# Four-stage transformer kernel, first block: sums and second scores ahead of the second QR broadcast, projection one tick later

## The chip, the cores and the metric

The kernel runs on one core of one Trainium2 chip, as one launch. The metric is the device time of that core in microseconds (us). Before the change it is 1303.81 us, the median of three runs (1302.42, 1303.81 and 1315.74).

## What is computed

The input is x, 32 sequences of 128 tokens with 144 channels, and one conditioning vector of 144 values for each sequence. Everything is float32. Four layers follow one another:

```
x = L0(x, cond)  # modulated attention (16 heads of 9, q and k normalised per head) + MLP 144-576-144
x = L1(x, cond)  # U = qr(P) of a 144x64 matrix; R = expm(A(cond)), A antisymmetric 64x64 per sequence
                 # x + ((x U) R - x U) U^T
x = L2(x, cond)  # modulated attention + MLP
x = L3(x, cond)  # modulated attention + mixture of 4 experts, top 2
```

In L0, q and k of each head of 9 values are divided by their standard deviation: y = (variance + eps)^-1/2. The kernel gets y from a guess made on the bit pattern of the variance (half the bits, subtracted from a constant) and three Newton steps.

## The kernel before, in words

**Tiling.** One sequence is one tile of 128 tokens (partitions) by 144 channels. The three attention layers (L0, L2, L3) are three "blocks", called layers 0, 1, 2 in the code, of 32 sequences each; the rotation L1 is done on the way from the first block to the second. The 144 channels are split into a main part of 128 and a rest of 16.

**Ticks and gaps.** The order of the work is written out by hand. A loop over `tick` starts at -6; each tick carries three sequences through attention: s0 = the sequence whose scores are computed with a first, unshifted product (`ps_s`, whose row maxima `nm` are taken by DVE, line 861), s1 = the one of the tick before, whose shifted scores (`ps_w`) go through the exponential on ACT (line 868), and s2 = the one of two ticks before, whose probabilities are multiplied with the values (`weigh`), normalised and projected. Between these fixed steps lie named gaps (a, e, t, stats, b0, b, den, pre1, c, y1, y2, y3, d, z); `fill(tick, gap)` puts into a gap what was registered for it. All engines work off their own instructions in the order in which this loop issues them, and wait for each other by semaphores.

**The order of a tick of the first block, before:** the deferred residual add (`sums_later`, POOL); gap a; e; t; first half of the scores (24 matmuls on PE, two maxima on DVE, two exponentials on ACT); stats; `weigh` (32 matmuls, a copy on ACT); b0; b; den; `sums` (two transposes on PE, reciprocal and a copy on DVE); second half of the scores (as the first); c; `divide_T` (two transposes on PE); y1; `divide` (DVE, makes oT); y2; y3; d; `largest_T` (one transpose, `ps_nm`) and `largest` (DVE, makes q2); z; `project_out` (two matmuls written `ps_pj`, each counted twice in the profile as float32 goes through PE in two passes) and `project_sum` (a product `res_a` on DVE, line 936; the add into x_sb on POOL, line 933, is put off to the start of the next tick).

**The QR in the gaps.** The QR of P is 64 Householder columns, one after the other, and each comes in three pieces (`prep_qr`, lines 318 to 356): piece 1 broadcasts a row of `at` on PE (line 327), squares and sums it on ACT (line 338), takes the root on POOL (line 339) and copies the row on ACT (line 340); piece 2 is five small DVE instructions (lines 342 to 349); piece 3 is the DVE update of `at` (line 353), which the broadcast of the next column reads. In the ticks 0 to 28 of the first block two columns are done in a tick. I call them A and B. `prepare_qr` (line 1196) puts piece 1 of A into gap a, pieces 2 and 3 of A into gap t, piece 1 of B into gap den, piece 2 of B into y1 and piece 3 into y2.

**What else lies in the gaps.** The matrix exponential (`prep_expm`) takes one piece in gap b and one in gap z of each tick until about tick 23; a piece is either a group of 32 or 64 small PE products with an ACT copy, or one or two DVE instructions over 128x1024 elements (the series). The layer norm's statistics (`ln_stats`: two small DVE instructions for each of two sequences, then seven on POOL) lie in gap e; the Newton steps in b, c and y2 on POOL; the MLP of a group of four sequences from ten ticks on after the group's first (`mlp1` in two parts, three 512-wide chunks in gaps stats and b, two chunks in gap d; `mlp2` in gaps b and d of the two ticks behind these).

**PSUM.** All matmul results but the attention output take the next of seven banks in turn; a bank is free again when its readers of seven allocations before are done.

The edit touches `ln_stats` (line 619), `qk0_guess` (line 754), `prepare_qr` (line 1196), the registration of the statistics and transposes of kind m (line 1253 on), and the loop over ticks (line 1368 on).

Of the kernel before, what the change touches and what calls it, by code (L numbers as in the profile page):

```python
# [10 lines left out]
I32 = mybir.dt.int32  # L11
AF = mybir.ActivationFunctionType
ALU = mybir.AluOpType
# [53 lines left out]
def tile_kernel(ctx: ExitStack, tc: tile.TileContext, a: dict, out: bass.AP):  # L67
# [551 lines left out]
    def ln_stats(pairs):  # L619

        n = len(pairs)
        name = "_".join(f"{kind}{s}" for s, kind in pairs)
        mv = small.tile([128, n, 2], F32, tag="mv", name=f"mv_{name}")
        for k, (s, kind) in reversed(list(enumerate(pairs))):
            bs = small.tile([128, 6], F32, tag="st", name=f"st_{kind}_{s}")
            nc.vector.bn_stats(bs, x_sb[:, of(s)[1], :])
            nc.vector.bn_aggr(mv[:, k, :], bs)  # L627
        rs = small.tile([128, 2, n], F32, tag="rs", name=f"rs_{name}")
        nc.gpsimd.tensor_scalar(rs[:, 0, :], mv[:, :, 1], 1.0, EPS, ALU.mult, ALU.add)  # L629
        nc.gpsimd.tensor_tensor(rs[:, 0, :], rs[:, 0, :], neghalf[:, :n], ALU.pow)  # L630
        nc.gpsimd.tensor_scalar(rs[:, 1, :], mv[:, :, 0], -1.0, 0.0, ALU.mult, ALU.add)
        for k, (s, kind) in enumerate(pairs):
            b = of(s)[1]
            minus, r = rs[:, 1, k : k + 1], rs[:, 0, k : k + 1]
            xh = work.tile([128, CM], F32, tag="xh", name=f"xh_{kind}_{s}", bufs=3)
            nc.gpsimd.tensor_scalar(xh, x_sb[:, b, :CM], minus, r, ALU.add, ALU.mult)
            xr = take_xr()
            nc.gpsimd.tensor_scalar(
                xr.rearrange("p (k c) -> p k c", k=4)[:, :, :CR],
                x_sb[:, b, CM:].unsqueeze(1).to_broadcast([128, 4, CR]),  # L640
                minus, r, ALU.add, ALU.mult,
            )
            st[s][f"xh_{kind}"], st[s][f"xr_{kind}"] = xh, xr

    def ln_T(s, kind):
# [108 lines left out]
    def qk0_guess(s):  # L754
        va = st[s]["va"]
        y = small.tile([128, 32], F32, tag="qky", name=f"qky_{s}", bufs=2)
        nc.vector.tensor_scalar(
            y.bitcast(I32), va.bitcast(I32), 1, None, ALU.logical_shift_right
        )
        nc.vector.tensor_scalar(y.bitcast(I32), y.bitcast(I32), -1, RSQRT, ALU.mult, ALU.add)  # L760
        st[s]["y"] = y

    def qk0_newton(s, eng=nc.gpsimd):
# [186 lines left out]
    def project_sum(s):  # L950
        layer, b, g, i = of(s)
        residual(b, st[s].pop("pj"), gr[g]["ga"][:, i, :], f"a_{s}", layer == 0)
# [243 lines left out]
    def prepare_qr(tick, gap):  # L1196


        nonlocal prep_qr, prep_last, qr_rest
        if late is not None:  # L1200
            return
        if qr_rest:
            if tick < 0:
                pieces = {"e": 1, "stats": 2}
            else:

                pieces = {"a": 1, "t": 2, "den": 1, "y1": 1, "y2": 1}
            for _ in range(pieces.get(gap, 0)):
                next(prep_qr)
                qr_rest -= 1  # L1210
        elif prep_qr:
            if next(prep_qr, 0) == 0:
                prep_qr = None
        elif prep_last is None and not prep_expm:
            prep_last = prep_rot(rot_T[0])
        elif prep_last and next(prep_last, 0) == 0:
            load_late()
# [17 lines left out]
    def put(tick, gap, f, *args):  # L1235
        gaps[tick, gap].append((f, args))
# [16 lines left out]
    for layer in range(3):  # L1253
        ahead = 5 if layer == 0 else 6
        for n in range(NG):
            g = (layer, n)
            t0 = first[layer] + n * G
            for i in range(G):
# [6 lines left out]
                    put(at_a - 1, "b", rotate_in, n)  # L1265
                    put(at_a - 1, "d", rotate, n)
                stats[at_a].append((s, "a"))
                stats[t0 + i + 3].insert(0, (s, "m"))
                if layer < 2:
                    put(*((at_a, "d") if at_a != t0 + i - ahead else (at_a + 1, "b")), ln_T, s, "a")  # L1270
                else:
                    put(at_a, "d", ln_T, s, "a")
                if layer == 0:
                    put(t0 + i + 4, "a", ln_T, s, "m")
                else:
                    put(t0 + i + 3, "d", ln_T, s, "m")
                if layer == 0:
# [77 lines left out]
    def fill(tick, gap):  # L1355
        prepare_qr(tick, gap)
        while (tick, gap) == (last_prep, "b0") and late is None:
            prepare_qr(tick, gap)
            prepare_expm(tick, gap)

        if gap == ("t" if tick < 0 else "e" if tick < first[1] else "stats") and tick in stats:
            ln_stats(stats.pop(tick))
        for f, args in gaps.pop((tick, gap), ()):
            f(*args)
        prepare_expm(tick, gap)

    last_prep = first[1] - 5
    for tick in range(-6, first[2] + B + 14):
        s0, s1, s2 = (at_tick.get(tick - k) for k in range(3))
        for layer in range(3):  # L1370
            for n in range(NG):
                if tick == first[layer] + n * G:
                    gr[layer, n]["ga"] = load_gates(layer, n, 0)
                if tick == first[layer] + n * G + (6 if layer else 9):
                    gr[layer, n]["gm"] = load_gates(layer, n, 1)
        while sums_later:
            sums_later.pop()()
        fill(tick, "a")
        fill(tick, "e")
        fill(tick, "t")  # L1380
# [3 lines left out]
            weigh(s2)  # L1384
        fill(tick, "b0")
        fill(tick, "b")
        fill(tick, "den")
        joined = tick >= first[1]
        if s2 is not None and not joined:
            sums(s2)  # L1390
        fill(tick, "pre1")
        if s2 is not None and joined:
            sums_by_blocks(s2)
        scores(s0, s1, 1)
        fill(tick, "c")
        if s2 is not None and not joined:
            divide_T(s2)
        fill(tick, "y1")
# [15 lines left out]
        fill(tick, "z")  # L1414
        if joined:
            fill(tick, "d")
        if s2 is not None and not ahead:
            project_out(s2)
            project_sum(s2)
    assert not gaps and not stats, (sorted(gaps), sorted(stats))  # L1420
# [164 lines left out]
```

## Time and profile before

The profile is of one execution that took 1303.81 us; its span from the first to the last instruction is 1302.1 us, so 1.7 us lie around it. That execution is also the median of the three.

| what | from | value |
|---|---|---|
| PE, DVE, ACT, POOL busy | part 1 of the page | 97%, 62%, 64%, 53% of the span |
| granted TensorE clock, mean | cores view | 0.993 |
| first block, ticks 0 to 28 (37 to 381 us) | broadcasts of line 327 in the timeline | 344 us |
| broadcast of column A to that of B, tick 8 | timeline | 121.00 to 126.15 us |
| broadcast of B to that of the next A, tick 8 | timeline | 126.15 to 131.44 us |
| the guess of the inverse root, two DVE instructions, tick 8 | timeline, lines 757 and 760 | 0.15 and 0.22 us |
| rest of the normalised x, 128x64, POOL | timeline, line 638 | 0.39 us |

The length of each of the ticks 0 to 28, from one broadcast of column A to the next (for tick 28, whose QR column is the last, to the transpose `ps_nm`), in us:

```
tick    0    1    2    3    4    5    6    7    8    9
      11.4 10.5  9.7 12.3 10.6 10.5  9.5  9.5 10.4 10.8
tick   10   11   12   13   14   15   16   17   18   19
      13.3 12.2 12.2 12.1 12.0 14.2 11.5 12.3 13.3 13.7
tick   20   21   22   23   24   25   26   27   28
      13.0 12.9 13.3 13.4 11.0 10.5 12.0 11.4  9.8
```

How to read it: a matmul's end is modelled, so PE counts as busy somewhat longer than it works. Idle time is only shown with what ended it. A line like `[0.97 <-DVE oT L926]` says that the engine had been idle for 0.97 us and that DVE's oT, line 926, set it free. In the waits view a line gives the engine and the line that waited, what for, the sum in us, how often, and the longest.

### The profile page before, as it was taken

The page shows a single profiled execution, that of the slowest core. Times are in us where ns is not written, and L with a number is a line of the kernel's source. Part 1 is how long each engine was busy: PE and PEld are TensorE (multiplying, and loading weights), DVE is VectorE, ACT ScalarE, POOL GpSimd, SP SyncE. Part 2 cuts the span into 40 slices and gives each one's busy share as a digit, 9 for nine tenths or more (in the row PEclk, how much of TensorE's full clock was granted, in tenths as well). Part 3 has the DMA queues.
Part 4 walks back from the last instruction along what each step waited for, and adds up shares of the span by engine and source line. Part 5 has one row for each costly group of instructions (what it writes and reads, how often), then busy time and mean ns, then how long its engine had stood idle before and what let it go on. Part 6 is the DMA issues. An engine that isn't in the chain of part 4 may idle for free.

```text
span 1302.1 us, 35663 instructions
## 1 busy us (share of the span) xinstructions
PE 1259.5 (97%) x14180; PEld 920.3 (71%) x14180; DVE 807.7 (62%) x2534; ACT 833.4 (64%) x1832; POOL 690.4 (53%) x1667
## 2 busy tenths in 40 slices
PE   6989898999999999999999999999999999999998
PEld 4678676786776667767777766767676767677666
DVE  5698888876774457667666666646464646455343
ACT  3568677678767566777767777665656555555431
POOL 5667777665753345445445554746464636361610
PEclk9999999999999999999999999999999999999999
DMA  8200000000003000000110000200000000000000
GB/s 234 62 2 21 20 7 15 20 3 22 20 2 134 19 11 21 11 20 20 37 29 20 20 11 11 76 11 19 11 20 11 19 11 19 11 19 2 19 10 10
DMA packets 21720, 34.43 MB, mean 26 GB/s; under 512 B 2353, under 2 KB 12497, under 8 KB 21297
## 3 DMA queue, kind: packets, MB, share of 16 engines
q1 hardware_dynamic: 20896, 31.70, 8.1%
q8 instruction: 114, 1.87, 0.6%
q10 hardware_dynamic: 656, 0.42, 0.2%
q14 instruction: 54, 0.43, 0.1%
HBM read 29.65 MB, written 2.47 MB: 25 GB/s over the span
## 4 chain that ended last, share of the span: by engine, by line
PE 71%; DVE 3%; ACT 1%; issue 0%; POOL 0%; DVEq 0%; POOLq 0%
PE ps_h L668 19%; PE ps_f L1118 10%; PE ps_s L856 7%; PE ps_qk L668 6%; PE ps_w L856 6%; PE ps_o L883 5%; PE ps_f L977 5%; PE ps_pj L947 3%; PE ps_v L668 2%; PE ps_f L1123 1%; PE ps_o L815 1%; DVE nm L861 1%; PE ps_z L1009 1%; PE ps_hT_m L656 1%; PE ps_cw L1106 1%; PE ps_hT_m L655 1%
## 5 line engine op out<-in xcount | busy, mean ns | idle before, releaser
L861 DVE TENSOR_REDUCE nm<-ps_s 128x4 f32<-128x512 f32 x384 | 246.3, 682 | 89.4 <-PE ps_w L856 67.8
L868 ACT ACTIVATE pr<-ps_w 128x512 f32<-128x512 f32 x384 | 208.6, 595 | 106.1 <-PE ps_w L856 104.6
L856 PE MATMUL ps_s<-kT,qT 32*128 32x256 f32 x1536 | 228.4, 404 | 0.7 <-ACT kT L791 0.6
L856 PE MATMUL ps_w<-q,kT 32*128 32x128 f32 x3072 | 229.0, 283 | 0.0
L856 PEld LDWEIGHTS ps_w<-q,kT 32*128 32x128 f32 x3072 | 194.2, 187 | 9.8 <-issue 6.2
L971 ACT ACTIVATE hid<-ps_h 128x512 f32<-128x512 f32 (+1 forms) x224 | 120.0, 591 | 100.1 <-PE ps_h L668 99.6
L856 PEld LDWEIGHTS ps_s<-kT,qT 32*128 32x128 f32 x1536 | 134.5, 184 | 29.6 <-issue 8.6
L668 PE MATMUL ps_h<-hM_m,mlps 128*128 128x512 f32 x304 | 144.0, 607 | 0.0
L1127 DVE SCALAR_TENSOR_TENSOR acc<-ps_f,cw,acc 128x144 f32<-128x144 f32 x128 | 46.7, 366 | 149.5 <-PE ps_f L1118 74.3
L933 POOL TENSOR_TENSOR x_sb<-x_sb,res_a 128x144 f32<-128x144 f32 x96 | 47.1, 490 | 146.7 <-DVE res_a L936 145.9
L883 PE MATMUL ps_o<-pr,vaug 128*32 128x128 f32 x3072 | 104.2, 276 | 0.3 <-issue 0.3
L883 PEld LDWEIGHTS ps_o<-pr,vaug 128*32 128x32 f32 x3072 | 78.1, 109 | 33.4 <-PE ps_w L856 18.9
L668 PEld LDWEIGHTS ps_h<-hM_m,mlps 128*128 128x128 f32 x304 | 53.3, 189 | 67.5 <-issue 66.6
L734 POOL TENSOR_SCALAR kT<-kT,cst 128x512 f32<-128x512 f32 x40 | 62.4, 1564 | 61.5 <-ACT kT L721 60.5
L977 PE MATMUL ps_f<-mlps,hid 128*128 128x144 f32 x640 | 93.5, 293 | 0.0
L977 PEld LDWEIGHTS ps_f<-mlps,hid 128*128 128x128 f32 x640 | 82.4, 191 | 7.8 <-issue 3.2
L868 ACT ACT_TABLE_LOAD x57 | 73.1, 1283 | 6.5 <-PE ps_w L856 5.7
L629 POOL TENSOR_SCALAR rs_m_a<-mv_m_a 128x2 f32<-128x2 f32 x81 | 15.6, 193 | 114.4 <-DVE mv_m_a L627 86.1
L968 ACT ACT_TABLE_LOAD x58 | 74.4, 1283 | 1.0
L658 ACT ACTIVATE hM_m<-ps_hT_m,modM 128x128 f32<-128x128 f32 x96 | 44.7, 465 | 45.5 <-PE ps_hT_m L656 45.4
L1118 PEld LDWEIGHTS ps_f<-pair,hid 128*128 128x128 f32 x512 | 66.9, 190 | 8.4 <-issue 7.7
L1118 PEld LDWEIGHTS ps_f<-mlps,hid 128*128 128x128 f32 x512 | 66.7, 190 | 8.1 <-issue 7.2
(328 smaller groups left out, 2918.5 us busy)
## 6 DMA issues: line engine op xcount, KB each, us to landing
gates<-gates SPq DMA_DIRECT2D x48, 288.0 KB, 3.5
x_sb<-in_x SPq DMA_DIRECT2D x8, 288.0 KB, 9.2
out_x<-x_sb SPq DMA_DIRECT2D x7, 288.0 KB, 2.5
mlps<-in_L_mlp SPq DMA_DIRECT2D x2, 1000.0 KB, 6.2
pair<-in_L_mlp SPq DMA_DIRECT2D x1, 1800.0 KB, 11.8
mlps<-in_L_mlp SPq DMA_DIRECT2D x1, 1800.0 KB, 8.2
pow<-in_W SPq DMA_DIRECT2D x4, 320.0 KB, 6.5
mlps<-in_L_wmod SPq DMA_DIRECT2D x4, 290.0 KB, 4.8
```

The source lines that it names most:

```text
L668: nc.tensor.matmul(ps, x, y, start=k == 0, stop=k == 1)
L734: eng.tensor_scalar(o, k, m, None, ALU.mult)
L856: nc.tensor.matmul(o, x, y, start=True, stop=True)
L861: nc.vector.tensor_reduce(nmv[:, at0 : at0 + 2, ONE : ONE + 2], view.rearrange("p (r t k) -> p r t k", t=2, k=T), AX.X, ALU.max, negate=True,)
L868: nc.scalar.activation(pr[:, 4 * e : 4 * e + 4, :].rearrange("p s q -> p (s q)"), view, AF.Exp, scale=SCALE,)
L883: nc.tensor.matmul(po[rows4(j), t, :], v[:, 4 * j + 2 * t + r, :], prs[j // 2][:, 4 * (j % 2) + 2 * r + t, :], start=r == 0, stop=r == 1,)
L933: nc.gpsimd.tensor_tensor(x_sb[:, b, :], x_sb[:, b, :], t, ALU.add)
L968: nc.scalar.activation(t, half, AF.Gelu_apprx_tanh)
L971: nc.scalar.activation(hid[:n, i], ps[:n], AF.Gelu_apprx_tanh)
L977: nc.tensor.matmul(ps, hid[:, at0, i, :], w2[:, m, :], start=m == 0, stop=m == NFC - 1)
L1118: nc.tensor.matmul(ps[:, 0, :], hid[:, at0 + m, i, :], w2[:, at0 + m, :], start=m == 0, stop=m == 3)
L1127: nc.vector.scalar_tensor_tensor(acc, ps[:, 0, :], w, acc, ALU.mult, ALU.add)
```

## The change

- The deferred residual add on POOL moves from the start of the next tick to behind gap c.
- In the first block piece 1 of column B moves from gap den to the head of gap c, which lies behind the second half of the scores. `sums` now comes ahead of gap den.
- The projection of the first block is done one tick later (for the sequence of three ticks before instead of two), behind `sums` and ahead of the second scores, instead of at the end of the tick. Statistics and transposes of kind m, which read its sum, are a tick later too (4 and 5 instead of 3 and 4 ticks behind).
- The guess of the inverse root is one DVE instruction (times -0.5, plus constant) instead of two (shift; times -1, plus constant).
- The rest of the normalised x of kind a is written once in the first block (128x16) instead of four times (128x64).

```
--- before.py
+++ after.py
@@ -635,11 +635,12 @@
             xh = work.tile([128, CM], F32, tag="xh", name=f"xh_{kind}_{s}", bufs=3)
             nc.gpsimd.tensor_scalar(xh, x_sb[:, b, :CM], minus, r, ALU.add, ALU.mult)
             xr = take_xr()
-            nc.gpsimd.tensor_scalar(
-                xr.rearrange("p (k c) -> p k c", k=4)[:, :, :CR],
-                x_sb[:, b, CM:].unsqueeze(1).to_broadcast([128, 4, CR]),
-                minus, r, ALU.add, ALU.mult,
-            )
+            if s < B and kind == "a":
+                o, rest = xr[:, :CR], x_sb[:, b, CM:]
+            else:
+                o = xr.rearrange("p (k c) -> p k c", k=4)[:, :, :CR]
+                rest = x_sb[:, b, CM:].unsqueeze(1).to_broadcast([128, 4, CR])
+            nc.gpsimd.tensor_scalar(o, rest, minus, r, ALU.add, ALU.mult)
             st[s][f"xh_{kind}"], st[s][f"xr_{kind}"] = xh, xr
 
     def ln_T(s, kind):
@@ -754,10 +755,7 @@
     def qk0_guess(s):
         va = st[s]["va"]
         y = small.tile([128, 32], F32, tag="qky", name=f"qky_{s}", bufs=2)
-        nc.vector.tensor_scalar(
-            y.bitcast(I32), va.bitcast(I32), 1, None, ALU.logical_shift_right
-        )
-        nc.vector.tensor_scalar(y.bitcast(I32), y.bitcast(I32), -1, RSQRT, ALU.mult, ALU.add)
+        nc.vector.tensor_scalar(y.bitcast(I32), va.bitcast(I32), -0.5, RSQRT, ALU.mult, ALU.add)
         st[s]["y"] = y
 
     def qk0_newton(s, eng=nc.gpsimd):
@@ -1204,7 +1202,7 @@
                 pieces = {"e": 1, "stats": 2}
             else:
 
-                pieces = {"a": 1, "t": 2, "den": 1, "y1": 1, "y2": 1}
+                pieces = {"a": 1, "t": 2, "c": 1, "y1": 1, "y2": 1}
             for _ in range(pieces.get(gap, 0)):
                 next(prep_qr)
                 qr_rest -= 1
@@ -1265,13 +1263,13 @@
                     put(at_a - 1, "b", rotate_in, n)
                     put(at_a - 1, "d", rotate, n)
                 stats[at_a].append((s, "a"))
-                stats[t0 + i + 3].insert(0, (s, "m"))
+                stats[t0 + i + 3 + (layer == 0)].insert(0, (s, "m"))
                 if layer < 2:
                     put(*((at_a, "d") if at_a != t0 + i - ahead else (at_a + 1, "b")), ln_T, s, "a")
                 else:
                     put(at_a, "d", ln_T, s, "a")
                 if layer == 0:
-                    put(t0 + i + 4, "a", ln_T, s, "m")
+                    put(t0 + i + 5, "a", ln_T, s, "m")
                 else:
                     put(t0 + i + 3, "d", ln_T, s, "m")
                 if layer == 0:
@@ -1373,8 +1371,6 @@
                     gr[layer, n]["ga"] = load_gates(layer, n, 0)
                 if tick == first[layer] + n * G + (6 if layer else 9):
                     gr[layer, n]["gm"] = load_gates(layer, n, 1)
-        while sums_later:
-            sums_later.pop()()
         fill(tick, "a")
         fill(tick, "e")
         fill(tick, "t")
@@ -1384,15 +1380,21 @@
             weigh(s2)
         fill(tick, "b0")
         fill(tick, "b")
-        fill(tick, "den")
         joined = tick >= first[1]
         if s2 is not None and not joined:
             sums(s2)
+        s3 = at_tick.get(tick - 3, B)
+        if s3 < B:
+            project_out(s3)
+            project_sum(s3)
+        fill(tick, "den")
         fill(tick, "pre1")
         if s2 is not None and joined:
             sums_by_blocks(s2)
         scores(s0, s1, 1)
         fill(tick, "c")
+        while sums_later:
+            sums_later.pop()()
         if s2 is not None and not joined:
             divide_T(s2)
         fill(tick, "y1")
@@ -1414,7 +1416,7 @@
         fill(tick, "z")
         if joined:
             fill(tick, "d")
-        if s2 is not None and not ahead:
+        if s2 is not None and s2 >= B and not ahead:
             project_out(s2)
             project_sum(s2)
     assert not gaps and not stats, (sorted(gaps), sorted(stats))
```

More of the change, by code (lines that the diff above doesn't have):

```diff
@@ L637, in ln_stats @@
             xr = take_xr()
[L638 to L642, printed above, removed]
+            if s < B and kind == "a":
+                o, rest = xr[:, :CR], x_sb[:, b, CM:]
+            else:
+                o = xr.rearrange("p (k c) -> p k c", k=4)[:, :, :CR]
+                rest = x_sb[:, b, CM:].unsqueeze(1).to_broadcast([128, 4, CR])
+            nc.gpsimd.tensor_scalar(o, rest, minus, r, ALU.add, ALU.mult)
             st[s][f"xh_{kind}"], st[s][f"xr_{kind}"] = xh, xr
@@ L756, in qk0_guess @@
         y = small.tile([128, 32], F32, tag="qky", name=f"qky_{s}", bufs=2)
[L757 to L760, printed above, removed]
+        nc.vector.tensor_scalar(y.bitcast(I32), va.bitcast(I32), -0.5, RSQRT, ALU.mult, ALU.add)
         st[s]["y"] = y
@@ L1205, in prepare_qr @@
             else:
-                pieces = {"a": 1, "t": 2, "den": 1, "y1": 1, "y2": 1}
+                pieces = {"a": 1, "t": 2, "c": 1, "y1": 1, "y2": 1}
             for _ in range(pieces.get(gap, 0)):
@@ L1267, in tile_kernel @@
                 stats[at_a].append((s, "a"))
-                stats[t0 + i + 3].insert(0, (s, "m"))
+                stats[t0 + i + 3 + (layer == 0)].insert(0, (s, "m"))
                 if layer < 2:
@@ L1273, in tile_kernel @@
                 if layer == 0:
-                    put(t0 + i + 4, "a", ln_T, s, "m")
+                    put(t0 + i + 5, "a", ln_T, s, "m")
                 else:
@@ L1375, in tile_kernel @@
                     gr[layer, n]["gm"] = load_gates(layer, n, 1)
-        while sums_later:
-            sums_later.pop()()
         fill(tick, "a")
@@ L1386, in tile_kernel @@
         fill(tick, "b")
-        fill(tick, "den")
         joined = tick >= first[1]
@@ L1390, in tile_kernel @@
             sums(s2)
+        s3 = at_tick.get(tick - 3, B)
+        if s3 < B:
+            project_out(s3)
+            project_sum(s3)
+        fill(tick, "den")
         fill(tick, "pre1")
@@ L1395, in tile_kernel @@
         fill(tick, "c")
+        while sums_later:
+            sums_later.pop()()
         if s2 is not None and not joined:
@@ L1416, in tile_kernel @@
             fill(tick, "d")
-        if s2 is not None and not ahead:
+        if s2 is not None and s2 >= B and not ahead:
             project_out(s2)
```

## Prediction

> **What bounds the kernel now.** The change touches the first block only, so I read the page (parts 1 and 4: PE is busy 97% and makes 71% of the chain that ended last), then the busy time by stretches, then the waits of that block, then single ticks in the timeline.
>
> ```profile
> core 0: us, PE busy (x) PEld busy (x) DVE busy (x) ACT busy (x) POOL busy (x), PEclk, DMA share, GB/s
> 37.00:69.00 32.00, 30.54 (x404) 21.78 (x406) 25.08 (x87) 19.41 (x58) 19.41 (x64) 1.00 0.22 53
> 69.00:142.00 73.00, 67.58 (x1023) 55.71 (x1024) 65.01 (x230) 52.40 (x154) 54.99 (x161) 0.98 0.04 10
> 142.00:381.00 239.00, 225.81 (x3079) 176.20 (x3081) 190.53 (x647) 179.18 (x470) 162.30 (x455) 0.99 0.05 15
> ```
>
> No engine is quite full here: PE idles 20 of 344 us, DVE has 281. From 69 to 142 us DVE is as full as PE. The waits of 37 to 381 us that the edit is after:
>
> ```profile
> PEld ps_pj L947 <- DVE oT L926: 8.6, 7, 1.3
> PE ps_qr L327 <- DVE at L353: 7.8, 6, 2.4
> PE ps_pj L947 <- DVE oT L926: 7.4, 8, 1.1
> DVE st_m L626 <- POOL x_sb L933: 6.0, 26, 0.7
> ```
>
> The first and third are the same stalls seen on PE's two halves: about 8 us for the projection, 8 us for the broadcast, 6 us of DVE. Next, tick 8 (121.00 to 131.44), one answer for each engine. PE, then DVE, ACT and POOL:
>
> ```profile
> 126.15 0.51 PE L327 MATMUL ps_qr<-at,cst 128*128 128x145 f32 x2
> 126.50 0.38 PE L896 MATMUL ps_o<-cst,on 128*128 128x128 f32 x2
> ...
> 127.92 0.66 PE L786 MATMUL ps_qkT<-cst,qkn 128*128 128x128 f32 x4
> ...
> 130.85 0.76 PE L947 MATMUL ps_pj<-L_wproj,oT 128*128 128x144 f32 x4 [0.97 <-DVE oT L926]
> 131.44 0.41 PE L327 MATMUL ps_qr<-at,cst 128*128 128x145 f32 x2
> ```
> ```profile
> 127.97 1.29 DVE L861 TENSOR_REDUCE nm<-ps_s 128x4 f32<-128x512 f32 x2 [0.40 <-PE ps_w L856]
> 129.18 0.15 DVE L342 SCALAR_TENSOR_TENSOR ala<-qrr,qr 128x1 uint32<-128x1 uint32 x1
> ...
> 130.71 0.33 DVE L353 SCALAR_TENSOR_TENSOR at<-qrr,qr,at 128x121 f32<-128x121 f32 x1
> ```
> ```profile
> 126.78 0.29 ACT L338 ACTIVATE qrk<-ps_qr 128x145 f32<-128x145 f32 x1
> ...
> 128.09 1.09 ACT L868 ACTIVATE pr<-ps_w 128x512 f32<-128x512 f32 x2 [0.76 <-PE ps_w L856]
> ```
> ```profile
> 127.24 0.55 POOL L339 TENSOR_TENSOR qr<-qr,half 128x1 f32<-128x1 f32 x1 [0.31 <-ACT qrk L338]
> ```
>
> To be seen: column B's square and root are done (127.79) while PE still computes the second scores and DVE waits for them. DVE starts B's five small instructions (129.18) right behind the two maxima. B's latency is hidden; the tick then ends by DVE: maxima, five instructions, oT, update (131.04), next broadcast.
>
> **The change part by part.** I call "sc" the moment at which PE is through with the second scores (127.92 in tick 8).
>
> *Broadcast B behind the second scores.* Now it starts at sc. ACT's order has the two exponentials ahead of the square: they end at 128.09+1.09 = sc+1.26. The square can overlap by 0.08 (as 129.06, the next ACT row, does); square and read-out take 0.38 (column A in the same tick: 121.51 to 121.89), hand-over 0.08, root 0.55, hand-over 0.28 (A: 122.60 to 122.87): DVE starts at sc+2.47, not at sc+1.26. From there to the end of the update it takes 1.86 as now (129.18 to 131.04), then 0.07: the next broadcast can go at sc+4.40. Before it went at sc+3.52. So DVE idles 1.2 us per tick, and a tick that this chain ends gets 0.88 longer there. Behind the square wait the q and k copies of ACT; behind the root wait eight Newton instructions, the residual add and the variance on POOL (some 1.3+0.5+1.3+0.25), which end at about sc+5.6, so column A's root starts some 0.2 later than its square allows (sc+5.44).
>
> *PE's own work behind sc* sets the end where it is longer than 4.40: broadcast 0.35, ps_qkT 0.49, ps_qk 0.97, rdx 0.22, ps_nm 0.20 = 2.23; and, where the tick has them, an exponential product 1.08, mlp2 1.23, mlp1 2.87 (starts of the rows of ticks 8, 20 and 27).
>
> *First half.* It loses the broadcast (126.15 to 126.50, 0.35) and gets the projection (130.85 to 131.44, 0.59): +0.24. The projection's wait for oT is gone, as oT is a tick old.
>
> *Residual add, statistics.* DVE no longer waits for x_sb (6.0/26 = 0.23 a tick), nor does column A's root stand behind the add, which stands behind res_a, itself behind the 1.0 to 1.3 us series pieces. That only helps where column A's update and the maxima behind it set the pace of the first half, through the banks.
>
> *Guess.* 0.15+0.22 becomes one instruction that the trace does not show; bounds 0.15 and 0.22, I take 0.22 (same form as line 760). *128x16 rest:* between 0.19 (128x2, line 629) and 0.39; I take 0.22, near the small rows. Both gains lie on DVE and POOL beside the chain above: nothing where column B ends the tick, up to 0.3 together where the first half waits for DVE. At worst, 0.
>
> Tick by tick: new end = old sc + 0.24 + the larger of 4.40 and PE's own work.
> - 5, 6, 7, 8 (no MLP): 6.9, 6.0, 5.9, 6.9 + 4.64 = 11.5, 10.6, 10.5, 11.5 against 10.5, 9.5, 9.5, 10.4: **+4.4**.
> - 13, 24, 25, 28 (mlp2 behind sc, no product: 3.46 < 4.40): 0.88+0.24 = 1.12 each: **+4.5**.
> - 10, 14, 18, 22, 26 (mlp1 in the first half, only 2.2 to 3.3 behind sc): here the exponentials also reload their table, 1.28 us, issued when ACT's previous work is done. In tick 14 the previous work ends at 200.21 (199.74+0.47), the exponentials then end at 202.58, 1.7 behind the new sc (200.58-0.25+0.59 = 200.92), not 1.26: +0.4; in 18 and 22 +0.2. So +0.88+0.24+0.3 = 1.4 each: **+7.0**.
> - 12, 16, 17, 20, 21 (PE has 4.54 behind sc with mlp2 and a product, or DVE with its series is the bound): ticks 20 and 21 gain 0.59 and lose 0.60; 12 and 17 gain about 0.4 each from column A, 16 loses 0.1: **-0.5**.
> - 11, 15, 19, 23, 27 (mlp1 behind sc: at least 5.1, so column B is hidden). Column A sets the first half: in tick 11 its DVE start moves from 3.3 to 2.8 behind the broadcast, in 15 from 3.8 to 2.9, in 27 from 2.8 to 2.1, in 19 some 0.6; PE's end loses the projection and gets the broadcast (-0.24). I take -0.7, -2.6, -0.9, 0, -0.8: **-5.0** (tick 15 carries 1.7 of a halved clock, below).
> - 0 to 4 and 9: DVE (matrix set-up) or the modulations are the bound, half of the loss counts: **+1.8**.
> - Ticks 29 to 34: no QR, the projection's stall there (0.8 in tick 28 to 29) and some DVE wait go: **-1**.
>
> Sum: 4.4+4.5+7.0-0.5-5.0+1.8-1 = +11.2 on the profiled execution's 1303.81 (span 1302.1 and 1.7 around it), which is the median: 1315.0.
>
> **The clock.** Rows first: in tick 15 PE stood still and then ran slow.
>
> ```profile
> 209.74 0.30 PEld L327 LDWEIGHTS ps_qr<-at,cst 128*128 128x128 f32 x2 [2.65 <-issue]
> ```
> ```profile
> 210.00:212.00 2.00, 2.00 (x29) 1.61 (x29) 2.00 (x4) 0.67 (x4) 1.83 (x5) 0.80 0.01 4
> 212.00:216.00 4.00, 4.00 (x13) 2.71 (x13) 3.71 (x13) 3.29 (x8) 3.33 (x11) 0.67 0.01 2
> ```
>
> The granted clock fell to a half for about 3.4 us after an idle time of 2.65 us; ps_qkT and ps_qk took 2.83 (211.74 to 214.57) instead of 1.46. That cost about 1.7 with the scores ahead. The new order opens an idle time of 2.2 to 2.5 us at the end of ticks 9, 10, 14 and 26 (4.4 to 4.7 less 2.23). I count none of them in the sum (tick 9 to 10 has a slow stretch already); four would be +6.8.
> The Trainium skill, "TensorE: Matmul & The Clock Gate", section "What's actually happening", has it that the clock halves after an idle window of about 3.4 us. By that rule none of the new idle times would halve it and the sum stays; by the row above, with 2.65 us enough, some will.
>
> **The rivals.**
> - *The clock falls* in three or more of those ticks: +11 and 3 to 5 times 1.7 = 1320 to 1324. For: the row above, and idle times almost as long. Against: 0.97 to 1.24 us idle at the ends of ticks 8, 10 and 14 left the clock whole.
> - *About even*: column A's earlier start is worth more in ticks 9 to 19, where DVE's series makes POOL's add and root late (0.5 more in ten ticks), and ticks 0 to 4 lose nothing: +11-5-2 = 1308, down to 1300.
> - *Faster*: the moved broadcast stays hidden. It decides at sc+1.26: if B's root were there when the maxima are done, the second half would be 0.88 shorter than I have it in about 15 ticks (-13, and -1.5 for the table), and the stalls (8+8) would be free: 1315-14.5-13 = about 1288. For: the waits table. Against: ACT works in order, and its two exponentials end at the very moment at which DVE is done with the maxima; nothing can overtake them.
> - *The change does little*: not possible for the order, it is written out; the waits can only move.
>
> **How the numbers follow.** Forecast (1309 to 1320) 0.50; clock 0.20; even (1297 to 1309) 0.21; faster than 1297 0.09. About 1% is what a measurement of this kernel can tell from no change: 1290.8 and 1316.8. Of the forecast 0.27 lie below 1316.8, 0.23 above. Faster by over 1%: 0.06. Within: 0.27+0.21+0.03 = 0.51. Slower: 0.23+0.20 = 0.43. The range 1301 to 1325 leaves out the "faster" case, some of "even" below it, and a clock that falls more than four times. For the forecast alone it is 1309 to 1320.
>
> **What would show it.** Right: in ticks 5 to 8 DVE idles about 1.2 us between the maxima and line 342, waiting for POOL's root; the exponentials stand ahead of the square; ticks of 11.5 and 10.6; PE idles ahead of broadcast A in ticks 13, 14, 24 to 26; no wait of ps_pj for oT and none of st_m for x_sb; ticks 20 and 21 unchanged at 13. Wrong: ticks 5 to 8 not longer; ticks 11, 15, 27 not shorter; more slow stretches of the clock than before.

## The result, and the profile after

The changed kernel takes 1324.02 us in the median of four runs (1319.52, 1319.77, 1328.27, 1329.04), beside 1306.10 us of the kernel before in four (1302.42 to 1315.74). The ratio is 1.012, with a 95% interval of 1.0077 to 1.0163: some 1% slower (16 us by the ratio, 18 by the medians). The prediction was 1315, and 1301 to 1325 as its range. The profiled execution took 1319.52 us (span 1317.8, granted clock 0.992 against 0.993 before), 15.7 more than that of before.

The busy time by stretches first (columns as in the prediction; the block begins at 36.3 us here, and its tick 28 ends at 389.0 instead of 376.2; so the 37 to 381 us of before hold 4.8 us behind tick 28, its ticks 0 to 28 take 339.3 us together, and tick 28 took 9.6, not 9.8).

```profile
core 0: us, PE busy (x) PEld busy (x) DVE busy (x) ACT busy (x) POOL busy (x), PEclk, DMA share, GB/s
37.00:69.00 32.00, 29.97 (x409) 21.76 (x411) 25.12 (x84) 18.99 (x60) 19.09 (x62) 1.00 0.21 53
69.00:142.00 73.00, 64.57 (x986) 53.52 (x982) 60.25 (x208) 47.61 (x140) 51.60 (x145) 0.95 0.03 10
142.00:389.00 247.00, 227.48 (x3085) 177.72 (x3082) 187.74 (x616) 180.15 (x478) 165.33 (x458) 0.99 0.04 14
```

PE now idles 2.0 + 8.4 + 19.5 = 30 us in these stretches instead of 20 (18.4 up to the end of tick 28); DVE is less full too. So neither got more work: both wait. For what, the waits of 37 to 391 us say:

```profile
POOL qr L339 <- ACT qrk L338: 67.7, 34, 5.8
DVE ala L342 <- POOL qr L339: 28.2, 40, 1.4
PE ps_qr L327 <- DVE at L353: 25.0, 17, 2.6
...
PEld ps_qk L690 <- DVE res_a L934: 4.5, 6, 1.3
...
PE ps_qk L690 <- DVE res_a L934: 3.0, 4, 1.1
```

Two of them before the change:

```profile
POOL qr L339 <- ACT qrk L338: 17.8, 13, 3.6
DVE ala L342 <- POOL qr L339: 2.9, 3, 1.9
```

Read from the bottom of the chain upwards: the broadcast of the next column A (PE, line 327) waits 25.0 us for the update (line 353), where it waited 7.8 before; DVE's five instructions wait 28.2 us for POOL's root (2.9 before), and the root waits 67.7 us for ACT's square (17.8 before; POOL's idle time as such costs nothing). The stalls that the change was after are gone (no wait of `ps_pj` for oT, none of `st_m` for `x_sb`), and a new one has come: `ps_qk` waits for `res_a`, whose product on DVE still holds the projection's PSUM bank.

Tick 8 (123.79 to 135.34), PE, DVE, ACT and POOL:

```profile
130.98 0.51 PE L327 MATMUL ps_qr<-at,cst 128*128 128x145 f32 x2
131.33 0.60 PE L784 MATMUL ps_qkT<-cst,qkn 128*128 128x128 f32 x4
...
132.96 0.27 PE L813 MATMUL ps_nm<-cst,nm 128*128 128x128 f32 x1
135.34 0.59 PE L327 MATMUL ps_qr<-at,cst 128*128 128x145 f32 x2 [2.11 <-DVE at L353]
135.73 0.42 PE L656 MATMUL ps_hT_m<-cst,xh_m 128*128 128x128 f32 x1
```
```profile
131.04 1.29 DVE L859 TENSOR_REDUCE nm<-ps_s 128x4 f32<-128x512 f32 x2 [0.68 <-PE ps_w L854]
133.17 0.20 DVE L342 SCALAR_TENSOR_TENSOR ala<-qrr,qr 128x1 uint32<-128x1 uint32 x1 [0.84 <-POOL qr L339]
```
```profile
131.16 1.08 ACT L866 ACTIVATE pr<-ps_w 128x512 f32<-128x512 f32 x2 [1.44 <-PE ps_w L854]
132.12 0.30 ACT L338 ACTIVATE qrk<-ps_qr 128x145 f32<-128x145 f32 x1
```
```profile
132.59 0.55 POOL L339 TENSOR_TENSOR qr<-qr,half 128x1 f32<-128x1 f32 x1 [2.61 <-ACT qrk L338]
```

To be seen: PE has column B's row ready from about 131.4 on (its next product starts at 131.33), but ACT takes up the square at 132.12, behind the two exponentials; the root ends at 133.14; DVE has waited 0.84; the next broadcast goes at 135.34, 4.36 behind the end of the second scores (130.98), and PE has stood still for 2.11.

All 29 ticks, length after minus length before (us):

```
tick     0     1     2     3     4     5     6     7     8     9
      -0.1   0.0  +0.3  -0.8  +1.0  +1.1  +1.0  +1.0  +1.1  +1.0
tick    10    11    12    13    14    15    16    17    18    19
      +0.4  -0.5  +0.3  +0.7  +1.6  -1.8  +0.4  +0.3  +1.1  -0.4
tick    20    21    22    23    24    25    26    27    28
      +0.1  +0.1  +1.9  -1.0  +0.9  +1.0  +1.6  +0.4  +1.0
```

Sum of ticks 0 to 28 +13.5; the eight ticks behind them +3.5; start and rest of the program -1.2. Together 15.8, the difference of the two executions but for rounding. Three windows of halved clock lie in these ticks of either profile: before in ticks 3, 10 and 15, after in ticks 4, 9 and 27.

### The profile page after: what moved, and what is told of

The parts are those of the page before. It is cut to its first block, busy times and chain, and to the rows that moved or that the text cites. A ratio compares the mean times of both kernels' runs of the same rounds, so it can differ in the third digit from the quotient of the medians.

```text
span 1317.8 us, 35607 instructions
## 1 busy us (share of the span) xinstructions
PE 1261.1 (96%) x14180; PEld 923.2 (70%) x14180; DVE 804.2 (61%) x2502; ACT 830.8 (63%) x1832; POOL 692.5 (53%) x1667
## 3 DMA queue, kind: packets, MB, share of 16 engines
HBM read 29.65 MB, written 2.47 MB: 24 GB/s over the span
## 4 chain that ended last, share of the span: by engine, by line
PE 69%; DVE 3%; ACT 2%; issue 1%; POOL 0%; DVEq 0%; POOLq 0%; ACTq 0%
PE ps_h L669 19%; PE ps_f L1116 9%; PE ps_s L854 7%; PE ps_qk L669 6%; PE ps_w L854 6%; PE ps_o L881 6%; PE ps_f L975 5%; PE ps_pj L945 3%; PE ps_v L669 2%; PE ps_f L1121 1%; PE ps_o L813 1%; DVE nm L859 1%; PE ps_hT_m L656 1%; PE ps_hT_m L657 1%; PE ps_cw L1104 1%
## 5 line engine op out<-in xcount | busy, mean ns | idle before, releaser
L881 PE MATMUL ps_o<-pr,vaug 128*32 128x128 f32 x3072 | 106.9, 281 | 0.1
L881 PEld LDWEIGHTS ps_o<-pr,vaug 128*32 128x32 f32 x3072 | 80.1, 112 | 33.2 <-PE ps_w L854 18.9
L975 PEld LDWEIGHTS ps_f<-mlps,hid 128*128 128x128 f32 x640 | 82.4, 191 | 7.8 <-issue 3.8
L339 POOL TENSOR_TENSOR qr<-qr,half 128x1 f32<-128x1 f32 x64 | 35.0, 548 | 77.5 <-ACT qrk L338 75.7
```

What stands on the lines that cost most here:

```text
L881: nc.tensor.matmul(po[rows4(j), t, :], v[:, 4 * j + 2 * t + r, :], prs[j // 2][:, 4 * (j % 2) + 2 * r + t, :], start=r == 0, stop=r == 1,)
L975: nc.tensor.matmul(ps, hid[:, at0, i, :], w2[:, m, :], start=m == 0, stop=m == NFC - 1)
```

## The experiments

An execution of one and the same kernel varies by some 16 us here (32 runs of the kernel before: 1303.4 to 1319.7). So each experiment is read twice: by its times, and by the ticks of its profile against those of before. "Ticks 1 to 28" is the change of that stretch's sum; tick 0 is left out, as it took 11.2 to 21.0 us in the profiles with the clock's start (in one of them, of 18.9 us, the clock was halved from 30.8 to 54.7 us). The numbers of the kernels below are those of this table's rows.

| kernel | median us | before, same job | ratio, 95% interval | ticks 1 to 28, us |
|---|---|---|---|---|
| 1: column B back in gap den | 1315.1 | 1310.9 | 1.0016 [0.9987, 1.0046] | -1.3 |
| 2: only column B moved | 1326.9 | 1310.9 | 1.0094 [1.0057, 1.0131] | +11.6 |
| 3: changed kernel, square first | 1320.3 | 1310.9 | 1.0061 [1.0037, 1.0084] | +7.6 |
| 4: only the guess and the rest | 1308.4 | 1310.9 | 0.9967 [0.9938, 0.9996] | -4.0 |
| 5: only the late add | 1305.9 | 1310.1 | 0.9960 [0.9933, 0.9988] | -5.0 |
| 6: late add, guess, rest | 1304.3 | 1310.1 | 0.9953 [0.9926, 0.9981] | -7.5 |
| 7: as 6, projection behind the scores | 1302.8 | 1310.1 | 0.9951 [0.9920, 0.9982] | -6.0 |
| 8: as 7, oT behind the update | 1302.4 | 1310.1 | 0.9924 [0.9897, 0.9950] | -2.8 |
| 9: as 8, add behind gap den | 1305.0 | 1310.8 | 0.9959 [0.9930, 0.9988] | -4.9 |
| 10: as 6, add behind gap den | 1304.3 | 1310.8 | 0.9966 [0.9934, 0.9999] | -7.3 |

**Theory:** the loss is column B's broadcast behind the second scores: its square stands behind the exponentials on ACT, and B's latency is no longer hidden. **Rivals:** the loss lies in the projection, in the late add, or in the clock.

**1. Column B back in its old place**, all else as changed.

```diff
-                pieces = {"a": 1, "t": 2, "c": 1, "y1": 1, "y2": 1}
+                pieces = {"a": 1, "t": 2, "den": 1, "y1": 1, "y2": 1}
```

> The changed kernel with one part undone: the broadcast of column B back in gap den, ahead of the second scores; sums first, projection a tick later, short guess and short rest stay. Theory (the moved broadcast exposes column B's latency): nearly all of the loss goes. A tick of the kind of 5 to 8 has the broadcast (0.35) and the projection (0.59) in its first half, sc 0.59 later than in the kernel before, and ends by DVE at sc+3.24 (no projection between): +0.3 against before; ticks 11, 15, 19, 27 stay shorter. Sum 0 to -4 us against before: ratio 0.995 to 1.002, profile near 1303; DVE goes from the maxima straight to line 342. Rival (the later projection and statistics cost the time): it stays 8 us or more above before, ratio over 1.006.

Measured: ratio 1.0016, so most of the loss goes with this one line. But ticks 5 to 8 stay 0.6, 0.3, 0.4 and 0.6 longer than before: something else costs there too. Experiments 6 and 10 name it.

**2. Only column B moved**, all else as before: the same line turned round in the kernel before ("den" to "c").

> The kernel before with that one part done: piece 1 of column B in gap c instead of den; everything else as before. Theory: first half 0.35 shorter; oT is 1.21 later, so the projection runs from about sc+4.14 and the next broadcast goes at sc+4.73 instead of sc+3.52: +0.86 in a tick that column B ends, more in the ticks with a table reload, nothing where PE is full: +10 to +14 us, ratio 1.008 to 1.011. Rival (the projection's place costs the time): within 3 us of before, ratio under 1.003.

Measured: ratio 1.0094, ticks 1 to 28 +11.6. Ticks 5 to 8 get 0.7 to 1.0 longer, ticks 10, 14, 18, 22 and 26 together 6.7; ticks 20 and 21 not at all. The theory holds from both sides: this part alone makes most of the slow-down.

**3. The square ahead of the exponentials.** Column B stays behind the second scores, but piece 1 is issued between their matmuls and their maxima and exponentials, so that ACT does the square first.

```diff
-    def scores(s, w, n):
+    def scores(s, w, n, mid=None):
...
+        if mid is not None:
+            mid()
...
-                pieces = {"a": 1, "t": 2, "c": 1, "y1": 1, "y2": 1}
+                pieces = {"a": 1, "t": 2, "mid": 1, "y1": 1, "y2": 1}
...
-        scores(s0, s1, 1)
+        scores(s0, s1, 1, (lambda: prepare_qr(tick, "mid")) if qr_rest else None)
```

> The changed kernel, but piece 1 of column B is issued between the second scores' matmuls and their maxima and exponentials: on PE it is at the same place, on ACT the square and the row's copy come ahead of the two exponentials. Theory (ACT's order costs most of it): root done at sc+1.55, DVE starts line 342 at sc+1.83 instead of sc+2.47, next broadcast at sc+3.76: -0.64 in ticks that column B ends, -0.9 in those with a table reload; about -10 us against the changed kernel, ratio to before 1.002 to 1.007. Rival (the place on PE behind the scores costs it, whatever ACT does): as the changed kernel, ratio 1.010 to 1.014. Second rival (the later exponentials cost what the square gains, through the q and k copies and the banks): above 1.010 although DVE starts line 342 earlier.

Tick 8 of this kernel on DVE, and ACT from the end of tick 26 into tick 27:

```profile
137.03 1.29 DVE L861 TENSOR_REDUCE nm<-ps_s 128x4 f32<-128x512 f32 x2 [0.68 <-PE ps_w L854]
138.62 0.20 DVE L342 SCALAR_TENSOR_TENSOR ala<-qrr,qr 128x1 uint32<-128x1 uint32 x1 [0.30 <-POOL qr L339]
```
```profile
366.25 0.29 ACT L338 ACTIVATE qrk<-ps_qr 128x145 f32<-128x145 f32 x1 [1.23 <-PE ps_qr L327]
...
366.83 1.28 ACT L868 ACT_TABLE_LOAD   x1
368.12 1.09 ACT L868 ACTIVATE pr<-ps_w 128x512 f32<-128x512 f32 x2
...
370.44 0.46 ACT L746 ACTIVATE qksq<-ps_qk 128x288 f32<-128x288 f32 x1
```

DVE's idle time falls from 0.84 to 0.30, and ticks 5 to 8 are 2.35 shorter together than in the changed kernel. So ACT's order is the cause of about half of the loss there, shown by taking it away. It is all that column B's place costs in these ticks: they stay 1.83 longer than before, and kernel 1, with column B in its old place, keeps 1.91. But the whole kernel gains little (1.0061 against 1.012), and the second answer shows where it is given back: with the square first, the table for the exponential is loaded behind it (366.83), where the changed kernel loads it 0.6 ahead of the end of the second scores (361.26 and 361.87), mostly in ACT's idle time; the exponentials, the q and k copies and the squares `qksq` come later, the variance on POOL waits for these, and the next column A's root stands behind the variance. Ticks 11, 15, 19, 23 and 27 are 5.3 us longer together than in the changed kernel.

**4. Only the guess in one instruction and the 128x16 rest** (those two hunks of the change in the kernel before).

> The kernel before with only the guess in one instruction and the rest of kind a written once. Theory: the new guess takes 0.15 to 0.22 us, so DVE has 0.15 less per tick, POOL 0.2 less; off the path in most ticks: 0 to -3 us, ratio 0.997 to 1.001. Rival (DVE bounds the ticks, so each of its instructions counts): -0.3 in each of 29 ticks, -9 us, ratio 0.993.

Measured: ratio 0.9967. Ticks 11, 12, 16, 17, 19 and 27 get 0.2 to 0.3 shorter, ticks 5 to 8, 13, 14, 18, 20 to 22 and 26 change by less than 0.1: it counts only where DVE's queue or column A is late, as the prediction had it. By the trace the gain is the guess's, one instruction of 0.15 in place of 0.15 and 0.22 (the two parts were not run apart). The rest saves POOL little or nothing: it took 0.35 to 0.39 in 11 ticks and 0.64 in 16, where the 128x64 form took 0.39 to 0.43 and the prediction had 0.22. Tick 8, POOL and DVE:

```profile
139.38 0.64 POOL L643 TENSOR_SCALAR xr<-x_sb,rs_m_a 128x16 f32<-128x16 f32 x1
```
```profile
139.48 0.48 DVE L772 TENSOR_TENSOR qkn<-qkraw,qky 128x288 f32<-128x288 f32 x1
```

The 0.64 comes in each tick where DVE's line 772, which reads two tiles in SBUF, starts 0.1 us into the rest, and the rest ends some 0.06 behind that line; where line 772 starts 0.3 us into it, the rest takes 0.35.

Ticks 10 and 15 get 1.3 and 1.8 shorter, but not by this edit: in the profile of before the clock was halved there (windows of 3.4 us from 142.9 and 211.2 us), here it was not. That prices such a window at 1.3 to 1.5 us.

**5. Only the late add**: the residual add behind gap c, statistics and transposes of kind m a tick later, in the kernel before.

> The kernel before with one part alone: the residual add goes behind gap c, and statistics and transposes of kind m a tick later. Column B stays in gap den, the projection at the end of the tick. My theory: the shortening of ticks 11, 15, 19, 23 and 27 that the changed kernel shows (-0.4 to -1.8 each) comes from column A's root, which no longer stands behind the add on POOL: here the same ticks get 0.3 to 1 shorter (tick 15 by some 1.5 more when the clock stays whole), ticks 5 to 8, 13, 20, 21 stay within 0.1. Ticks 1 to 28 together -3 to -6, the median 1301 to 1305 beside 1306 of the kernel before. Rival: the shortening comes from the projection that leaves the end of the tick; then these ticks stay as before and the sum is 0.

Measured: ratio 0.9960. Ticks 11, 15, 19, 23 and 27: -0.6, -2.1 (1.5 of it the clock), -0.4, -0.6, -0.9; net -3.2 where the prediction had -5.0 with 1.7 of clock in it. The rival is out; the add and the statistics are not told apart. But ticks 14 and 26 get 0.3 longer, 5 to 8 by 0.1.

**6. Late add, guess and rest together**, column B and the projection as before.

> The changed kernel without two of its parts: column B back in gap den, the projection back at the end of the tick of its own sequence. The residual add, the statistics, the guess in one instruction and the 128x16 rest stay changed. Theory: the gain of the late add and of the short guess come together, and the +0.3 to +0.6 that ticks 5 to 8, 14, 22, 24 to 26 showed with column B in den and the projection ahead of the second scores goes, because it was the projection's: ticks 5 to 8 within 0.1 of the kernel before, ticks 1 to 28 some -5 to -9, the median 1298 to 1303. Rival: that loss was the add's or the statistics'; then ticks 5 to 8 stay 0.3 to 0.6 longer here too and the median is 1305 to 1310.

Measured: ratio 0.9953, faster than before. Against it experiment 1 has one edit more, the projection ahead of the second scores: its ticks 5 to 8, 14, 18 and 26 are 0.3 to 0.5 longer each, 28 by 1.0. Its sum over ticks 1 to 28 is 6.2 higher, of which 2.2 lie in ticks 3, 4 and 24, where a halved clock ran in it and none in this one. So the projection there costs about 4. Yet ticks 5 and 8 are 0.3 longer here than before, too, and 6 and 7 are not. Tick 8 on DVE and on POOL:

```profile
127.17 1.29 DVE L859 TENSOR_REDUCE nm<-ps_s 128x4 f32<-128x512 f32 x2 [0.65 <-PE ps_w L854]
128.38 0.49 DVE L342 SCALAR_TENSOR_TENSOR ala<-qrr,qr 128x1 uint32<-128x1 uint32 x1
128.91 0.17 DVE L346 SCALAR_TENSOR_TENSOR qrr<-qrr,ala 128x1 f32<-128x1 f32 x1
```
```profile
128.37 0.49 POOL L931 TENSOR_TENSOR x_sb<-x_sb,res_a 128x144 f32<-128x144 f32 x1
```

Line 342, 128x1, took 0.15 before. Here it starts 0.01 behind POOL's add and ends with it. In ticks 10, 14 and 26 the add catches line 347 instead: 0.55 for 0.22, begun 0.05 ahead of the add and ended 0.02 behind it.

**7. The projection behind the second scores.** Column B as before; the projection a tick later behind gap c; its product on DVE behind the update; kind m one tick later again.

```diff
-        s3 = at_tick.get(tick - 3, B)
-        if s3 < B:
-            project_out(s3)
-            project_sum(s3)
         fill(tick, "den")
...
         while sums_later:
             sums_later.pop()()
+        s3 = at_tick.get(tick - 3, B)
+        if s3 < B:
+            project_out(s3)
...
         fill(tick, "y2")
+        if s3 < B:
+            project_sum(s3)
```

> Column B in gap den as before, the rest as in the changed kernel, but the projection (still a tick later) stands behind the second scores instead of ahead of them, its product on DVE behind column B's update, and statistics and transposes of kind m one tick later again. Theory: behind the second scores PE waits for DVE in ticks 5 to 8 (2.2 us of its own work against 3.5), so that the projection's 0.59 is hidden there and the next broadcast no longer stands behind it (131.04 end of the update, 131.44 broadcast: 0.33 each): ticks 5 to 8, 13, 24, 25, 28, 10, 14, 18, 22, 26 get 0.3 shorter than in the kernel before, 20 and 21 stay or get up to 0.6 longer if PE is the bound there; with the late add -8 to -13 in ticks 1 to 28, the median 1294 to 1300. Rival: the product on DVE or the projection on PE lies on the path behind the second scores; then these ticks are as in the kernel before or longer and the median is 1300 to 1306.

Measured: 0.9951, as experiment 6; ticks 5 to 8 at 0.0, -0.2, -0.1 and +0.2, not -0.3. The projection itself is hidden now (PE waits 1.2 us for DVE ahead of the broadcast of tick 9), and the stall on oT is gone, but line 342 takes 0.49 here too in ticks 5 and 8: what the one gave, the other took. The median of 1302.8 lies in the rival's 1300 to 1306.

**8. The normalisation behind the update**: `divide(s2)` and `fill(tick, "y2")` change places in the kernel of 7.

> As the run with the projection behind the second scores, and the normalisation (oT on DVE) goes behind column B's update, since nothing needs it in this tick any more. Theory: the tick ends by DVE's chain of maxima, five instructions, oT and update, so that oT's 0.3 leaves the path: ticks 5 to 8, 13, 24, 25, 28 another 0.2 to 0.35 shorter, in all some -3 beside the run without it. Rival: with the projection there PE's own work (2.8 us behind the second scores) or column A's root on POOL is next; then no difference.

Measured: 0.9924, the lowest ratio of the study; its interval overlaps that of 7, and ticks 8, 14 and 26 are 0.2 to 0.3 shorter, 5 to 7, 13, 25 and 28 within 0.13: in those the rival, no difference, holds. The profiled execution itself met more halved clock (10.2 us within ticks 1 to 28 and 3.4 behind them, against 3.4 and 0 in 7), so its sum says less than its times.

**9 and 10. The add beside the maxima.** In 8, and in 6, the residual add goes from behind gap c to behind gap den.

```diff
         fill(tick, "den")
+        while sums_later:
+            sums_later.pop()()
...
         fill(tick, "c")
-        while sums_later:
-            sums_later.pop()()
```

> As the run with the normalisation behind the update, but the residual add on POOL goes from behind gap c to behind gap den, ahead of the second scores and their Newton steps. In that run's profile DVE's line 342 took 0.49 us instead of 0.15 where it started beside the add (0.49 us, 128x144), and began and ended with it. Theory: the two hold each other up, and now the add runs beside the maxima, which read PSUM: line 342 at 0.15 again, ticks 5 to 8, 10, 13, 14, 18 and 26 shorter by 0.3 each, 2 to 3 in all. Rival: line 342 was long for another reason, or the maxima are held up in its place; then these ticks stay within 0.1 of the run before.

> The same one move in the run that has only the late add, the later statistics, the short guess and the short rest (projection at the end of the tick, column B in gap den). Theory: ticks 5, 8, 10, 13, 14, 18 and 26, which had 0.3 more behind the second scores, give it back (-0.3 each, some -2 in all), ticks 6, 7, 20 and 21 stay; ticks 11, 15, 19, 23 and 27 keep their gain, because the add is still behind column A's root. Rival: the 0.3 came from the statistics that stand a tick later; then nothing changes.

Tick 8 of the second of them, DVE and POOL:

```profile
126.83 1.29 DVE L859 TENSOR_REDUCE nm<-ps_s 128x4 f32<-128x512 f32 x2 [0.65 <-PE ps_w L854]
128.03 0.15 DVE L342 SCALAR_TENSOR_TENSOR ala<-qrr,qr 128x1 uint32<-128x1 uint32 x1
```
```profile
126.83 0.49 POOL L931 TENSOR_TENSOR x_sb<-x_sb,res_a 128x144 f32<-128x144 f32 x1
```

Beside the maxima, which read PSUM, the add costs nothing: they take 1.29 as ever, line 342 is back at 0.15 there, line 347 at 0.22 in ticks 10, 14 and 26, and in 10 the ticks 5, 8, 10, 13, 14, 18 and 26 are 0.33 to 0.46 shorter, 6, 7, 20 and 21 unchanged. So the two did hold each other. In 9 ticks 8, 14 and 26 (-0.3 to -0.4) show it, 13 and 18 do not: the theory holds there in part. The time does not follow (0.9959 and 0.9966, unchanged within the intervals), and the ticks say where it goes: in 10, ticks 11, 15, 19, 23 and 27 are longer by 0.6, 0.4, 0.3, 0.3 and 0.4. In tick 27 the trace shows why: column A's root stands on POOL behind the variance (line 752), which waits for DVE's sum over ACT's `qksq`, so that an earlier broadcast of A does not start its root earlier. For the other four I take it to be the same. That these ticks keep their gain was expected and was wrong.

## Why the prediction was right, and where it was not

*The mechanism held, step by step; the number only just.* The median of 1324.02 lies 9 us above the forecast and 1 us inside the range, outside the narrower 1309 to 1320, and two of the four executions lie outside the range. The next broadcast was put at sc+4.40 and came at sc+4.36; behind sc the ticks 5 to 8, 13 and 24 got 0.80 to 0.83 longer (25: 0.72), for 0.88. DVE's start on column B was put at sc+2.47 and came at sc+2.19 in tick 8 (so it idles 0.84, not 1.2); its chain from there to the update's end took 2.01 instead of 1.86, and the broadcast came 0.16 behind the update instead of 0.07. That 4.40 was met so closely is luck: the hand-over from POOL to DVE, put at 0.28, took 0.03 (the 0.28 was read from column A in tick 8, where DVE was still busy with line 760, 122.75 for 0.22), and the two later steps were 0.24 longer than put. The first half got 0.17 to 0.27 longer in ticks 5 to 8, for 0.24. The ticks of 11.5 and 10.6 are there (11.55, 10.52, 10.52, 11.54). Group by group, predicted and measured, us:

| ticks | predicted | measured |
|---|---|---|
| 5 to 8 | +4.4 | +4.2 |
| 13, 24, 25, 28 | +4.5 | +3.6 |
| 10, 14, 18, 22, 26 | +7.0 | +6.6 |
| 12, 16, 17, 20, 21 | -0.5 | +1.1 |
| 11, 15, 19, 23, 27 | -5.0 | -3.4 |
| 0 to 4 and 9 | +1.8 | +1.4 |
| tail | -1 | +3.5 |

*The mis-sized term is the tail*, "Ticks 29 to 34: no QR, the projection's stall there (0.8 in tick 28 to 29) and some DVE wait go: -1": +3.5 came. PE there, behind the last QR column, and the busy time by stretches of the same place:

```profile
389.04 0.27 PE L813 MATMUL ps_nm<-cst,nm 128*128 128x128 f32 x1
390.16 0.30 PE L373 MATMUL ps_yr<-at,cst 64*64 64x64 f32 x2 [0.84 <-DVE at L353]
391.65 0.75 PE L380 MATMUL ps_uT<-v,y 64*64 64x144 f32 x4 [1.20 <-DVE v L369]
...
395.95 1.94 PE L881 MATMUL ps_o<-pr,vaug 128*32 128x128 f32 x32
```
```profile
388.00:391.00 3.00, 1.61 (x13) 1.25 (x12) 2.76 (x13) 1.45 (x5) 2.50 (x9) 1.00 0.01 3
391.00:398.00 7.00, 6.08 (x70) 4.81 (x72) 4.37 (x20) 1.94 (x5) 2.55 (x8) 0.54 0.01 2
```

Before, the projection stood between `ps_yr` and `ps_uT` and filled a part of this gap:

```profile
376.89 0.76 PE L947 MATMUL ps_pj<-L_wproj,oT 128*128 128x144 f32 x4
378.17 0.47 PE L380 MATMUL ps_uT<-v,y 64*64 64x144 f32 x4 [0.53 <-DVE v L369]
```

After, PE is idle for 0.84 and 1.20 us there, the granted clock falls to a half from 391.6 on for 6.8 us, and 32 products of `weigh` take 1.94 instead of 1.08. The runs tie the tail's length to that clock. In each profile, the halved time in the eight ticks behind tick 28, and their length against before:

| halved, us | kernels | longer by, us |
|---|---|---|
| 0 | 4, 6, 7, 9, 10 | -0.2, +0.3, +1.0, +1.0, 0.0 |
| 3.4 | 1, 8 | +2.0, +2.7 |
| 6.8 | changed, 2, 5 | +3.5, +3.4, +3.1 |
| 10.2 | 3 | +4.9 |

So the tail's +3.5 is mostly halved clock, about 0.5 us for each us of it. Without it, too, the forecast -1 did not come (-0.2 to +1.0). One part of that is shown: with the statistics a tick later, those of kind m of the last sequence fall into the first tick of the second block. POOL then normalises two tiles ahead of the copies that `ps_xR` needs, PE waits for these, and two transposes follow:

```profile
464.77 0.73 PE L998 MATMUL ps_xR<-cst,xr 128*128 128x128 f32 x4 [0.40 <-POOL xr L997]
```

From the second scores of that tick to the first of the next it is 5.15 us in the changed kernel and 5.15 to 5.62 in all others with later statistics, 4.24 before and in kernels 2 and 4: 0.9 that the prediction had not counted. That the missing projection caused the halved clock is not shown: kernels 2 and 5 have the projection in its old place and met it too; kernels 7 and 9 have it not and escaped. No run forces a window, and the medians hold the average.

What decides where one falls is in part to be read from the clock's records in the twelve profiles (from 67 us on). In each profile all halved stretches begin on one grid of 3.413 us, and its phase differs from profile to profile. PE's idle time within one stretch of the grid, at full clock, tells what is granted in the next:

| PE idle in the stretch, us | next one halved |
|---|---|
| under 0.7 | 0 of 4072 |
| 0.7 to 1.1 | 6 of 118 |
| 1.1 to 1.95 | 14 of 58 |
| over 1.95 | 6 of 6 |

In the tail of the changed kernel PE idled 1.96 us between 388.2 and 391.6. Why the same idle time between 0.7 and 1.95 halves the clock at one time and not at another stays open.

*The rival "the clock falls"* named the ends of ticks 9, 10, 14 and 26. The idle times came (2.10, 2.61, 2.61 and 2.58 us, for 2.2 to 2.5), but only the last was followed by a halved window. The grid tells why: it cut the 2.61 of ticks 10 and 14 into 1.24 and 1.37, and 1.83 and 0.78; of the 2.58 of tick 26 one stretch held 2.43, and it held all of the 2.11 at the end of tick 8, which the rival had not named. Within ticks 1 to 28 the halved time is 10.2 us in both profiled executions, so the forecast that counted none of the four was right in sum by luck: windows fell in new places (from 135.6, behind the 2.11 us of idle time at the end of tick 8, where the transpose at 135.73 took 0.42 instead of 0.27; from 367.7, behind tick 26) and no longer in old ones. The rule of the Trainium skill that I cited, "TensorE: Matmul & The Clock Gate", section "What's actually happening", has the length of a window right (3.413 us; all windows here last 3.41 us or a multiple). An idle window of its full length is not needed: 2.11 us at one stretch were enough, and so were 0.84 and 1.20 with two products between them. Here the measurement decides.

*The smaller misses.* Ticks 12, 16 and 17 were to gain from column A or stay, and lost 0.25 to 0.4 each: the projection in the first half takes PE's time, and in ticks 12 and 17 its bank is held until `res_a` is done (the new wait of `ps_qk`). I had priced the projection by PE's 0.24 alone, without who holds its bank; experiment 6 against 1 puts it at about 4 us in all. The gain of ticks 11, 15, 19, 23 and 27 was -3.4 in the changed kernel, where the late add alone gave -4.7: the same wait for the bank takes 0.36 and 0.95 in ticks 11 and 15, and tick 27 holds a halved window. The projection's place alone does not take it, as kernel 1 has -7.1 there. The 128x16 rest was put at 0.22 and took 0.35 to 0.64. And line 342 beside the add, 0.33, I did not see at all; the changed kernel does not pay it in ticks 5 to 8, since there DVE waits for the root meanwhile; it pays 0.07 in line 353, which runs beside the add (0.44, and 0.37 in kernel 2).

*The rivals "about even" and "faster"* fall with experiments 1 to 3: the broadcast does not stay hidden, and the kernel without its move is the faster one.

## What to carry to other kernels

A latency chain over several engines that hides behind other work has a place on every engine's queue: moving its head a few instructions on PE put its second link behind 1.1 us of exponentials on ACT, and cost 0.8 us in each tick where the chain ended the tick. Price each part by itself: three parts of this change (late add, guess, rest) were worth 0.5% together (0.9953; of the rest no gain is shown), and with the projection and the normalisation in other places the kernel came to 0.9924, which the intervals do not tell apart from it, while column B's move and the projection ahead of the scores turned the whole into 1.012. And where a repaired wait yields nothing, look at the next tick: column A there waited for ACT, however early its broadcast came.

## What the runs showed of the hardware

- A DVE instruction of 128x1 with two SBUF inputs (line 342) took 0.49 instead of 0.15 us when it started together with a 128x144 add of 0.49 us on POOL, and ended with it; started 0.15 us into the add it took 0.35 (kernels 9 and 10). The maxima, which read PSUM, took 1.29 with the add beside them as without it. It goes the other way too: POOL's 128x16 rest took 0.64 instead of 0.35 beside DVE's line 772 (0.48), and 1.73 in five ticks of kernel 6, until line 537 or 491 right behind line 772 (1.21) was done too. The Trainium skill, "GPSIMD Engine Reference", section "1. Specifications", names what fits: POOL shares its SBUF interfaces with VectorE, in contention with DVE instructions that have two SBUF inputs. The price here is that the one held back lasts until the end of the other. It need not be the one that started later: line 347 was held when it started 0.05 us ahead of the add and not at 0.06 (kernel 5), the rest when it started 0.1 ahead of line 772 and not at 0.3.
- The granted clock halves for 3.41 us at a time after less idle time than one such window, on a grid of that length: idle time that a grid line cuts in two did less (2.61 us and whole clock) than a shorter one in one piece (2.11 us and half). A window cost 1.3 to 1.5 us in full ticks and about 1.7 in the tail. The windows fall differently in each profile, and tick 0 took 11.2 to 21.0 us with the clock's start. I take these to be most of the difference between executions of one kernel; each kernel was profiled once, so that is not shown.
- The table load for the exponential (1.28 us) was mostly hidden where ACT idled ahead of the exponential (started 0.6 us ahead of the end of the second scores); one 0.29 us square put ahead of it moved it onto the path (started 1.2 behind their end, kernel 3).
